# A cross-attention and FFT-FFN layer in fp32: FFN transposes one step earlier, and a written-out order for the last two tiles

## The chip, the cores and the metric

The kernel runs on one core of one Trainium2 chip. The metric is device microseconds from start to end of one execution. A core has five engines that run side by side[...]: TensorE (PE: matmuls and transposes, with weight loads shown as PEld), VectorE (DVE), ScalarE (ACT), GpSimd (POOL) and SyncE (SP, which here only issues DMAs). In the trace each engine works through its instructions in the order in which the program gives them.

## The reference

All data are fp32: x is 2 x 2048 x 512, the encoder's rows are 2 x 128 x 512, and the mask gives each query row 128 keys. In shortened form:

```python
q = layernorm(x) @ wq + bq            # 16 heads of 32
k, v = enc @ wk + bk, enc @ wv + bv
s = (q @ k.T) / sqrt(32) * mask
s = where(s == 0, -1e9, s)
x = x + softmax(s) @ v @ wo + bo
x = x + real(ifft(fft(layernorm(x)) @ (wr + 1j * wi))) + bias
```

The FFT, the complex product and the inverse FFT are linear, so the kernel builds one real 512 x 512 matrix `m_ffn` at its start and each FFN is one product with it.

## The kernel before, in words

The 4096 rows are 8 **groups** of 512 rows, and each group is 4 **tiles** of 128 rows. A tile goes through a **slot**. In slot (i, t), group i's tile t has its scores and softmax computed, while PE fills the time with products of neighbouring groups: queries of group i+1 (chain `q`), the output projection of group i-1 (chain `o`), the FFN of groups i-1 and i-2 (chain `y`). The text calls the group being attended i, the one before it p, the one before that pp, and i+2 is nn.

A **chain** (`chain`, L192) is 4 accumulating 128x512 matmuls; fp32 shows each as two records in the trace, so one chain is 8 records. A product needs its left operand with the contracted dimension on the partitions, so rows are first transposed: `transpose_rows` (L181) is 4 PE transposes of 128x128 into one PSUM bank, and one copy from there to SBUF by ACT or DVE. Three kinds occur: `tp_a` (normalized rows for the queries, copied to `xnT`), `tp_f` (normalized rows for the FFN, copied to `nT`) and `tpw` (softmax weights, in `transposed_weights`, L363, copied to `pt`).

PSUM is dealt out by three pools: `ps_sc` has 2 buffers of two banks for scores (one for each half of the heads), `ps_tp` has 2 banks that take turns for all transposes, `ps_mm` has 2 banks that take turns for chains. A bank can be written again only after the copy or add that reads it.

The softmax of one half of the heads (class `Softmax`, L318) is four steps. `masked` (L328, DVE) multiplies the scores by the mask. `maxima` (DVE) is L335 (the replacement of zeros), L337 (minimum of each head) and L338 (scaling). `exponentials` (L344, ACT) is 8 exponentials. `divided` is the reciprocal L356 on DVE and the product L357 on POOL. The transposes `tpw` of a tile need the product L357 of both halves.

The FFN of a row tile starts when its projection is added to x (`Project.evict`, L428, DVE). Then come `ffn_statistics` (L203 and L204 on DVE, L207 and L208 on POOL, which make `rstd_f`), `ffn_norm` (L211 on DVE, `norm_f`, and L447 on POOL, which adds the bias to x), `ffn_transposes` (PE and a copy to `nT`), and the chain `y` with its final add (L491, DVE) and the store.

Tile hands out buffers and semaphores, but the order is written by hand (`manual_schedule`). The function `slot` (L712) lays a slot out as: scores; `masked` of half 0; adds left over from the slot before (`carried`); the lists `pool` and `early`; `maxima` of half 0; chain 1; the first two `tpw` groups of the tile before; exponentials of half 0; `masked` of half 1; the add of chain 1; `on_a`; `maxima` of half 1; `on_m`; chain 2; `mid_b`; the last two `tpw` groups; exponentials of half 1; `divided` of half 0; the add of chain 2; `on_b`; chain 3; `end`; `divided` of half 1; `on_c`. Everything that a list names goes to its engines' queues at that place. A loop runs groups 1 to 5 through four slots each (group 1's slot 0 is written out before it), then groups 6 and 7 are written out, with their own lists. After the last slot come the last chain `y` of group 6, the `tpw` of the last tile, the context of group 7, its four projections and its four FFNs.

Of the kernel before, what the change touches and what calls it, by code (L numbers as in the profile page):

```python
# [9 lines left out]
FP = mybir.dt.float32  # L10
# [4 lines left out]
P = 128  # L15
# [7 lines left out]
def kernel(  # L23
# [62 lines left out]
    HC = NC // 2  # L86
# [22 lines left out]
    last = ngroups - 1  # L109
# [35 lines left out]
    for b in range(B):  # L145
# [3 lines left out]
        c = b * HC  # L149
# [39 lines left out]
        else:  # L189
            eng.tensor_copy(dst, ps)  # L190

    def chain(name, lhs, rhs, width=D):  # L192

        ps = ps_mm.tile([P, D], FP, tag="mm", name=name)[:, :width]
        for c in range(NC):
            nc.tensor.matmul(  # L196
                ps, lhs(c), rhs(c), start=(c == 0), stop=(c == NC - 1)
            )
        return ps

    def statistics(xt, mv, name):
# [67 lines left out]
    class Queries:  # L269
# [5 lines left out]
        def pe(self):  # L275
            i, g = self.i, self.g
            if i not in qTs:
                qTs[i] = big_tile("qT", 2, f"qT_{i}")
            self.ps = chain(
                f"q_{i}_{g}",  # L280
                lambda c: wq[:, c, g * P : (g + 1) * P],
                lambda c: xnTs[i][:, c, self.first * P :],
                width=GQ - self.first * P,
            )
# [75 lines left out]

    pts = {}

    def transposed_weights(i, t, first, end, eng=None):  # L363
        if t == 0 and first == 0:
            pts[i] = [big_tile("pt", 6, f"pt_{i}_{g}") for g in range(NC)]
        ws = weights[i, t]
        for g in range(first, end):
            ps = ps_tp.tile([P, NR, P], FP, tag="tp", name=f"tpw_{i}_{t}_{g}")
            for r in range(NR):
                nc.tensor.transpose(  # L370
                    ps[:, r, :], ws[r // 2].w[:, (r % 2) * NC + g, :], ident
                )
            dst = pts[i][g][:, :, t * P : (t + 1) * P]
            if eng:
                eng.tensor_copy(dst, ps)
            else:
                nc.scalar.copy(dst, ps)  # L377
# [34 lines left out]
    class Project:  # L412
# [2 lines left out]
        def __init__(self, i, t):  # L415
            self.i, self.t = i, t

        def pe(self):
            i, t = self.i, self.t
            self.ps = chain(  # L420
                f"o_{i}_{t}",
                lambda c: cTs[i][:, c, t * P : (t + 1) * P],
                lambda c: wo[:, c, :],
            )

        def evict(self):
# [5 lines left out]
    def ffn_statistics(i, t):  # L432
        n = f"f{i}_{t}"
        mv = small.tile([P, 2], FP, tag="mvf", name=f"mv_{n}")
        rstd = small.tile([P, 1], FP, tag="rstdf", name=f"rstd_{n}")
        statistics(groups[i][:, t, :], mv, n)
        inverse_deviations(rstd, mv[:, 1:2])
        fstats[i, t] = mv, rstd
# [15 lines left out]
    class Ffn:  # L454
        def __init__(self, i, t):
            self.i, self.t = i, t

        def pe(self):
            nT = nTs.pop((self.i, self.t))
            self.ps = chain(  # L460
                f"y_{self.i}_{self.t}",
                lambda c: nT[:, c, :],
                lambda c: m_ffn[:, c, :],
            )

        def in_halves(self):
# [230 lines left out]
    carried = []  # L697

    def run(job):
        job.pe()  # L700
        job.evict()

    def call(work):
        for f, *args in work:
            f(*args)

    def begin(i, t):
        sc = scores(i, t)
        weights[i, t] = [Softmax(i, t, hf, sc[hf]) for hf in range(2)]
        return weights[i, t]  # L710
# [124 lines left out]
    w = begin(0, 0)  # L835
# [20 lines left out]
    w = begin(0, 1)  # L856
# [21 lines left out]
    w = begin(0, 2)  # L878
# [19 lines left out]
    w = begin(0, 3)  # L898
# [32 lines left out]
    w = begin(1, 0)  # L931
# [29 lines left out]
    for i in range(1, last - 1):  # L961
        p, pp, n, nn = i - 1, i - 2, i + 1, i + 2
        q = [Queries(n, g) for g in range(NC)]
        q_nn = Queries(nn, 0)
        o = [Project(p, t) for t in range(TG)]
        f_p = Ffn(p, 0)
        second = q[1:]
        if i > 1:
            f_pp = [Ffn(pp, t) for t in range(TG)]
            second = [q[2], q[3], f_pp[3]]  # L970

        def if_pp(*work):
            return list(work) if i > 1 else []

        if i > 1:
            load_rows(nn)
            load_mask(n)
            load_residual(p)
            slot(
                i,  # L980
                0,
                [f_pp[1], f_pp[2], q[1]],
                turned=(p, TG - 1),
                early=[(ffn_transposes, pp, 1), (ffn_transposes, pp, 2)],
                pool=[(relative, nn, t, nc.gpsimd) for t in range(TG)],
                on_b=[(ffn_norm, pp, 3), (query_statistics, nn, 0, 2)],
                on_c=[(query_statistics, nn, 2, TG)],
                end=[(context, p, 0, 2)],
            )
        slot(  # L990
            i,
            1,
            second,
            turned=(i, 0),
            early=[(context, p, 2, NC)] + if_pp((ffn_transposes, pp, 3)),
            pool=[(output_bias, p)],
            on_b=[(query_norm, nn, 0), (query_norm, nn, 1)],
        )
        slot(
            i,  # L1000
            2,
            o[:3],
            turned=(i, 1),
            early=[(query_transposes, nn, 0), (query_transposes, nn, 1)],
            on_b=[
                (ffn_statistics, p, 0),
                (query_norm, nn, 2),
                (query_norm, nn, 3),
                (ffn_norm, p, 0),
            ],  # L1010
            on_c=[(ffn_statistics, p, 1)],
        )
        slot(
            i,
            3,
            [o[3], f_p, q_nn],
            turned=(i, 2),
            early=[
                (query_transposes, nn, 2),
                (query_transposes, nn, 3),  # L1020
                (ffn_transposes, p, 0),
            ],
            on_a=[(ffn_statistics, p, 2)],
            on_b=[(ffn_statistics, p, 3), (ffn_norm, p, 1)],
            on_c=[(ffn_norm, p, 2)],
        )


# [2 lines left out]
    i, n, p, pp = last - 1, last, last - 2, last - 3  # L1031
# [3 lines left out]
    o = [Project(p, t) for t in range(TG)]  # L1035
    f = [Ffn(pp, t) for t in range(TG)]
    f_p = [Ffn(p, t) for t in range(TG)]
# [2 lines left out]
        0,  # L1040
        [f[1], f[2], q[1]],
        turned=(p, TG - 1),
        early=[(ffn_transposes, pp, 1), (ffn_transposes, pp, 2)],
        on_b=[(ffn_norm, pp, 3)],
        end=[(context, p, 0, 2)],
    )
# [4 lines left out]
        turned=(i, 0),  # L1051
        soon=True,
        early=[(context, p, 2, NC), (ffn_transposes, pp, 3)],
# [48 lines left out]
    w[1].maxima()  # L1102
    w[1].exponentials()
    w[0].divided()
    o[0].pe()
    carried.append(o[0].evict)
    w[1].divided()
    load_residual(last)
    slot(
        i,  # L1110
        2,
        o[1:],
        turned=(i, 1),
        on_a=[(ffn_statistics, p, 0), (ffn_statistics, p, 1), (ffn_norm, p, 0)],
        on_m=[(ffn_norm, p, 1)],
        end=[(ffn_transposes, p, 0, nc.vector), (ffn_statistics, p, 2)],
    )
    slot(
        i,
        3,  # L1120
        f_p[:3],
        turned=(i, 2),
        early=[(ffn_transposes, p, 1)],
        mid_b=[(ffn_transposes, p, 2)],
        on_a=[(ffn_norm, p, 2), (ffn_statistics, p, 3)],
        on_m=[(ffn_norm, p, 3)],
        end=[(ffn_transposes, p, 3, nc.vector)],
    )
    carried.pop()()
    output_bias(last)  # L1130
    run(f_p[3])
    for g in range(NC):
        transposed_weights(last, TG - 1, g, g + 1, nc.vector if g % 2 else None)
    context(last, 0, NC)
    o = [Project(last, t) for t in range(TG)]
    f = [Ffn(last, t) for t in range(TG)]
# [56 lines left out]
```

## Time and profile before

| what | us |
|---|---|
| median of 3 runs (lowest to highest) | 547.02 (546.65 to 547.3) |
| the profiled execution, its own time | 546.47 |
| its span in the trace | 544.7 |
| PE busy in the span | 528.8 (97%) |
| DVE, ACT, POOL busy | 431.5, 342.9, 329.5 |
| one group in the steady loop (start of slot 0's scores, 325.86 to 387.40) | 61.54 |

The difference between the profiled time and its span, 1.8 us, lies before the first and after the last instruction. Busy PE is modelled from starts, so the better reading is from start to start: in the timeline a chain of 8 records begins 3.44 us before whatever follows it, and a block of 4 transposes 0.44 us. Time beyond such steps is time in which PE waited.

### The profile page before, as it was taken

Reading aid. Unit: us, or ns where it says so; the run is one execution under the profiler, and the core shown is the slowest. Engines: PE = TensorE matmul, PEld = TensorE weight load, DVE = VectorE, ACT = ScalarE, POOL = GpSimd, SP = SyncE. Lnnn points to the kernel's source line nnn. Section 1 sums busy time; section 2 is a strip of 40 time slices with the busy share of each in tenths; the row PEclk is TensorE's granted clock in tenths of the full one; section 3 lists DMA queues with packets and bytes.
Section 4 is the critical chain, followed back from the end, with each engine's and each line's share of the span. In section 5 each row is a group of like instructions: output and inputs, shape, how many; then the busy total and the mean of one; then the engine's idle time right before and its main releaser. Section 6 shows DMA issues by size and latency. Waiting matters only on the chain.

```text
span 544.7 us, 8783 instructions
## 1 busy us (share of the span) xinstructions
PE 528.8 (97%) x3005; PEld 292.7 (54%) x3005; DVE 431.5 (79%) x616; ACT 342.9 (63%) x1300; POOL 329.5 (61%) x268
## 2 busy tenths in 40 slices
PE   8989999999999999999999999999999999998997
PEld 7745566455545554455545555455545555554444
DVE  4798878899887989889887989889857898798251
ACT  3376886776677666666677676666686667756210
POOL 3256759826994469626895369626664466765450
PEclk9999999999999999999999999999999999999999
DMA  8950202000600024000510024000312001201102
GB/s 310 384 213 1 78 15 84 1 0 2 203 31 2 20 81 152 0 21 1 194 40 0 21 62 171 1 21 0 117 40 71 27 20 55 83 1 40 39 0 78
DMA packets 22992, 36.49 MB, mean 67 GB/s; under 512 B 2202, under 2 KB 6562, under 8 KB 22948
## 3 DMA queue, kind: packets, MB, share of 16 engines
q1 hardware_dynamic: 22260, 34.75, 18.4%
q10 hardware_dynamic: 688, 1.18, 0.6%
q8 instruction: 24, 0.39, 0.3%
q14 instruction: 20, 0.16, 0.1%
HBM read 27.53 MB, written 8.39 MB: 66 GB/s over the span
## 4 chain that ended last, share of the span: by engine, by line
PE 79%; DVE 11%; ACT 6%; POOL 1%; issue 1%; DMA 1%; SPq 0%; ACTq 0%; DVEq 0%; POOLq 0%
PE o L196 18%; PE y L196 17%; PE q L196 16%; PE tpw L370 8%; PE sc L309 5%; PE c L392 5%; ACT w L344 4%; DVE w L335 3%; DVE nmax L337 2%; PE tp_f L186 2%; DVE w L328 2%; PE tp_a L186 2%; PE k L535 1%; PE v L196 1%; DMA enc<-in_ctx_dram 1%
## 5 line engine op out<-in xcount | busy, mean ns | idle before, releaser
L344 ACT ACTIVATE w<-w,nmax 128x128 f32<-128x128 f32 x512 | 198.3, 395 | 19.2 <-DVE nmax L338 17.3
L357 POOL TENSOR_TENSOR w<-w,rden 128x1024 f32<-128x1024 f32 x64 | 123.7, 1933 | 120.0 <-DVE rden L356 59.9
L196 PE MATMUL o<-wo,cT 128*128 128x512 f32 x256 | 115.1, 594 | 0.0
L196 PE MATMUL y<-m_ffn,nT 128*128 128x512 f32 x248 | 112.4, 596 | 2.3 <-ACT nT L188 1.2
L196 PE MATMUL q<-xnT,wq 128*128 128x512 f32 (+1 forms) x256 | 112.0, 582 | 2.6 <-ACT qT L287 1.5
L377 ACT COPY pt<-tpw 128x512 f32<-128x512 f32 x122 | 65.6, 587 | 65.2 <-PE tpw L370 65.2
L344 ACT ACTIVATION_READ_ACCUMULATOR w<-w,nmax 128x1 f32 x512 | 99.4, 194 | 0.0
L335 DVE SCALAR_TENSOR_TENSOR w<-w 128x1024 f32<-128x1024 f32 x64 | 89.8, 1404 | 0.9
L328 DVE TENSOR_TENSOR w<-sc,mask 128x1024 f32<-128x1024 f32 x64 | 77.4, 1210 | 10.3 <-PE sc L309 9.9
L337 DVE TENSOR_REDUCE nmax<-w 128x8 f32<-128x1024 f32 x64 | 78.1, 1220 | 2.2
L370 PEld LDWEIGHTS tpw<-ident,w 128*128 128x128 f32 x512 | 59.4, 141 | 34.9 <-issue 29.3
L196 PEld LDWEIGHTS q<-xnT,wq 128*128 128x128 f32 x256 | 46.3, 190 | 48.6 <-issue 40.2
L196 PEld LDWEIGHTS o<-wo,cT 128*128 128x128 f32 x256 | 46.3, 190 | 47.9 <-issue 46.6
L196 PEld LDWEIGHTS y<-m_ffn,nT 128*128 128x128 f32 x248 | 44.7, 190 | 48.7 <-issue 44.8
L370 PE MATMUL tpw<-ident,w 128*128 128x128 f32 x512 | 67.9, 274 | 2.5 <-ACT nT L188 1.0
L447 POOL TENSOR_TENSOR x<-x,bf 128x512 f32<-128x512 f32 x32 | 48.9, 1528 | 18.3 <-DVE norm_f L211 18.3
L356 DVE RECIPROCAL rden<-den 128x8 f32<-128x8 f32 x64 | 12.7, 198 | 45.7 <-ACT w L344 45.7
L408 POOL TENSOR_TENSOR x<-x,bo 128x512 f32<-128x512 f32 x32 | 47.2, 1507 | 0.0
L309 PEld LDWEIGHTS sc<-kT,qT 32*128 32x128 f32 x1024 | 31.5, 186 | 21.0 <-issue 18.8
L228 POOL TENSOR_SCALAR rel<-rows 128x512 f32<-128x512 f32 x26 | 42.0, 1630 | 1.2 <-PE tp_a L186 1.2
L207 POOL TENSOR_SCALAR rstd_f<-mv_f 128x1 f32<-128x1 f32 x32 | 20.0, 625 | 34.8 <-DVE mv_f L204 34.8
L188 ACT COPY nT<-tp_f 128x512 f32<-128x512 f32 x30 | 17.1, 585 | 34.5 <-PE tp_f L186 34.4
(95 smaller groups left out, 535.1 us busy)
## 6 DMA issues: line engine op xcount, KB each, us to landing
rows<-in_x_dram SPq DMA_DIRECT2D x32, 256.0 KB, 4.7
x<-in_x_dram SPq DMA_DIRECT2D x32, 256.0 KB, 4.9
out_dram<-x SPq DMA_DIRECT2D x31, 256.0 KB, 2.0
mask<-in_mask_Bx1xSxS_fk_dram SPq DMA_DIRECT2D x8, 256.0 KB, 5.2
wk<-in_L_xattn_wk_w_dram ACTq DMA_DIRECT2D x2, 512.0 KB, 6.2
wq<-in_L_xattn_wq_w_dram SPq DMA_DIRECT2D x1, 1024.0 KB, 7.2
wr<-n_L_ffn_w_freq_real_dram SPq DMA_DIRECT2D x2, 512.0 KB, 5.2
wi<-n_L_ffn_w_freq_imag_dram SPq DMA_DIRECT2D x2, 512.0 KB, 7.7
```

The lines of the kernel that those rows point to most:

```text
L196: nc.tensor.matmul(ps, lhs(c), rhs(c), start=(c == 0), stop=(c == NC - 1))
L228: eng.tensor_scalar(d, xt, xt[:, 0:1], None, ALU.subtract)
L309: nc.tensor.matmul(sc[r // 2][:, r % 2, g, :], qTs[i][rows, g, t * P : (t + 1) * P], kT[rows, g, b * K : (b + 1) * K], start=True, stop=True,)
L328: nc.vector.tensor_tensor(self.w, self.sc.rearrange("p r g k -> p (r g) k"), self.mrow, ALU.mult)
L335: nc.vector.scalar_tensor_tensor(w, w, 0.0, w, ALU.is_equal, ALU.subtract)
L337: nc.vector.tensor_reduce(self.nmax, w, AX.X, ALU.min)
L344: nc.scalar.activation(w[:, h, :], w[:, h, :], AF.Exp, bias=self.nmax[:, h : h + 1], scale=-UNIT, accum_out=self.den[:, h : h + 1],)
L357: nc.gpsimd.tensor_tensor(w, w, rden.unsqueeze(2).to_broadcast([P, HH, K]), ALU.mult)
L370: nc.tensor.transpose(ps[:, r, :], ws[r // 2].w[:, (r % 2) * NC + g, :], ident)
L377: nc.scalar.copy(dst, ps)
L408: nc.gpsimd.tensor_tensor(xs[:, t, :], xs[:, t, :], bo, ALU.add)
L447: nc.gpsimd.tensor_tensor(xt, xt, bf, ALU.add)
```

## The change

The change has four parts.

1. In the loop, `(ffn_transposes, p, 0)` moves from slot 3's `early` to the end of slot 2, and `(ffn_transposes, pp, 1)` moves from the next group's slot 0 `early` to the end of slot 3 (also for group 6's slot 0). In slot 2 the statistics of tile 0 go from `on_b` to `on_a`, and its norm goes ahead of two query norms. In slot 3 the norm of tile 1 goes ahead of the statistics of tile 3.
2. `chain` takes `between`: work that is issued after its second matmul. For the last tiles it puts a whole `ffn_transposes` in the middle of a chain.
3. Slots 2 and 3 of group 7 are written out instead of using `slot`: `masked` of tile 2 now stands ahead of `divided` of tile 1's second half, and `maxima`, exponentials, norms and statistics stand in another order.
4. The last tile's four `tpw` groups go into the two score buffers (four banks) instead of through the two banks of `ps_tp`.

No operation is added or removed; SP's queue of DMA issues is the same, in the same order. The diff, cut to its core:

```diff
+    def chain(name, lhs, rhs, width=D, between=()):
...
+            if c == HC - 1:
+                call(between)
...
             ps = (
+                banks[g]
+                if banks
+                else ps_tp.tile([P, NR, P], FP, tag="tp", name=f"tpw_{i}_{t}_{g}")
             )
...
# loop, slot 0 (and the same in group 6)
-                early=[(ffn_transposes, pp, 1), (ffn_transposes, pp, 2)],
+                early=[(ffn_transposes, pp, 2)],
# loop, slot 2
-            on_b=[
-                (ffn_statistics, p, 0),
-                (query_norm, nn, 2),
-                (query_norm, nn, 3),
-                (ffn_norm, p, 0),
-            ],
+            on_a=[(ffn_statistics, p, 0)],
+            on_b=[(ffn_norm, p, 0), (query_norm, nn, 2), (query_norm, nn, 3)],
             on_c=[(ffn_statistics, p, 1)],
+            end=[(ffn_transposes, p, 0)],
# loop, slot 3
-            early=[
-                (query_transposes, nn, 2),
-                (query_transposes, nn, 3),
-                (ffn_transposes, p, 0),
-            ],
+            early=[(query_transposes, nn, 2), (query_transposes, nn, 3)],
             on_a=[(ffn_statistics, p, 2)],
-            on_b=[(ffn_statistics, p, 3), (ffn_norm, p, 1)],
+            on_b=[(ffn_norm, p, 1), (ffn_statistics, p, 3)],
             on_c=[(ffn_norm, p, 2)],
+            end=[(ffn_transposes, p, 1)],
# group 7 (i = 7, p = 6), from the first projection on
-    o[0].pe()
-    carried.append(o[0].evict)
-    w[1].divided()
-    load_residual(last)
-    slot(i, 2, o[1:], turned=(i, 1),
-        on_a=[(ffn_statistics, p, 0), (ffn_statistics, p, 1), (ffn_norm, p, 0)],
-        on_m=[(ffn_norm, p, 1)],
-        end=[(ffn_transposes, p, 0, nc.vector), (ffn_statistics, p, 2)])
-    slot(i, 3, f_p[:3], turned=(i, 2),
-        early=[(ffn_transposes, p, 1)],
-        mid_b=[(ffn_transposes, p, 2)],
-        on_a=[(ffn_norm, p, 2), (ffn_statistics, p, 3)],
-        on_m=[(ffn_norm, p, 3)],
-        end=[(ffn_transposes, p, 3, nc.vector)])
-    carried.pop()()
+    run(o[0])
+    ffn_statistics(p, 0)
+    load_residual(last)
+    old = w
+    w = begin(i, 2)
+    w[0].masked()
+    old[1].divided()
+    o[1].pe()
+    w[0].maxima()
+    ffn_norm(p, 0)
+    transposed_weights(i, 1, 0, HC)
+    w[0].exponentials()
+    w[1].masked()
+    o[1].evict()
+    ffn_statistics(p, 1)
+    w[1].maxima()
+    o[2].pe()
+    transposed_weights(i, 1, HC, NC)
+    w[1].exponentials()
+    ffn_norm(p, 1)
+    w[0].divided()
+    o[2].evict()
+    ffn_statistics(p, 2)
+    o[3].pe(between=[(ffn_transposes, p, 0, nc.vector)])
+    ffn_transposes(p, 1)
+    w[1].divided()
+    w = begin(i, 3)
+    w[0].masked()
+    o[3].evict()
+    ffn_statistics(p, 3)
+    ffn_norm(p, 2)
+    f_p[0].pe()
+    w[0].maxima()
+    transposed_weights(i, 2, 0, HC)
+    w[0].exponentials()
+    w[1].masked()
+    f_p[0].evict()
+    f_p[1].pe(between=[(ffn_transposes, p, 2, nc.vector)])
+    ffn_norm(p, 3)
+    w[1].maxima()
+    transposed_weights(i, 2, HC, NC)
+    f_p[1].evict()
+    w[0].divided()
+    w[1].exponentials()
+    f_p[2].pe(between=[(ffn_transposes, p, 3, nc.vector)])
+    f_p[2].evict()
+    w[1].divided()
     output_bias(last)
     run(f_p[3])
+    free = [
+        ps_sc.tile([P, 2, NC, K], FP, tag="sc", name=f"tpw_last_{hf}")
+        for hf in range(2)
+    ]
+    banks = [free[g // 2][:, g % 2] for g in range(NC)]
     for g in range(NC):
-        transposed_weights(last, TG - 1, g, g + 1, nc.vector if g % 2 else None)
+        transposed_weights(
+            last, TG - 1, g, g + 1, nc.vector if g % 2 else None, banks
+        )
```

More of the change, by code (lines that the diff above doesn't have):

```diff
@@ L190, in transpose_rows, with call @@
             eng.tensor_copy(dst, ps)
-    def chain(name, lhs, rhs, width=D):
+    def call(work):
+        for f, *args in work:
+            f(*args)
+    def chain(name, lhs, rhs, width=D, between=()):
         ps = ps_mm.tile([P, D], FP, tag="mm", name=name)[:, :width]
@@ L361, with transposed_weights @@
     pts = {}
-    def transposed_weights(i, t, first, end, eng=None):
+    def transposed_weights(i, t, first, end, eng=None, banks=None):
         if t == 0 and first == 0:
@@ L367, in transposed_weights @@
         for g in range(first, end):
-            ps = ps_tp.tile([P, NR, P], FP, tag="tp", name=f"tpw_{i}_{t}_{g}")
+            ps = (
+                banks[g]
+                if banks
+                else ps_tp.tile([P, NR, P], FP, tag="tp", name=f"tpw_{i}_{t}_{g}")
+            )
             for r in range(NR):
@@ L416, in __init__, with pe @@
             self.i, self.t = i, t
-        def pe(self):
+        def pe(self, between=()):
             i, t = self.i, self.t
@@ L423, in pe @@
                 lambda c: wo[:, c, :],
+                between=between,
             )
@@ L456, in __init__, with pe @@
             self.i, self.t = i, t
-        def pe(self):
+        def pe(self, between=()):
             nT = nTs.pop((self.i, self.t))
@@ L463, in pe @@
                 lambda c: m_ffn[:, c, :],
+                between=between,
             )
@@ L701, in run @@
         job.evict()
-    def call(work):
-        for f, *args in work:
-            f(*args)
     def begin(i, t):
@@ L1042 @@
         turned=(p, TG - 1),
-        early=[(ffn_transposes, pp, 1), (ffn_transposes, pp, 2)],
+        early=[(ffn_transposes, pp, 2)],
         on_b=[(ffn_norm, pp, 3)],
@@ L1104 @@
     w[0].divided()
-    o[0].pe()
-    carried.append(o[0].evict)
-    w[1].divided()
-    load_residual(last)
[L1109 to L1113, printed above, removed]
-        on_a=[(ffn_statistics, p, 0), (ffn_statistics, p, 1), (ffn_norm, p, 0)],
-        on_m=[(ffn_norm, p, 1)],
[L1116 to L1122, printed above, removed]
-        early=[(ffn_transposes, p, 1)],
-        mid_b=[(ffn_transposes, p, 2)],
-        on_a=[(ffn_norm, p, 2), (ffn_statistics, p, 3)],
-        on_m=[(ffn_norm, p, 3)],
-        end=[(ffn_transposes, p, 3, nc.vector)],
-    )
-    carried.pop()()
+    run(o[0])
[23 more added lines that the diff above has]
+    ffn_transposes(p, 1)
+    w[1].divided()
+    w = begin(i, 3)
[19 more added lines that the diff above has]
+    w[1].divided()
     output_bias(last)
     run(f_p[3])
+    free = [
[3 more added lines that the diff above has]
+    banks = [free[g // 2][:, g % 2] for g in range(NC)]
     for g in range(NC):
-        transposed_weights(last, TG - 1, g, g + 1, nc.vector if g % 2 else None)
+        transposed_weights(
+            last, TG - 1, g, g + 1, nc.vector if g % 2 else None, banks
+        )
     context(last, 0, NC)
```

## The prediction

> **What bounds the kernel now.** I read the page's busy shares and its chain that ended last, then who waited for whom on PE, then PE's timeline around each wait.
>
> ```profile
> span 544.7 us, 8783 instructions
> PE 528.8 (97%) x3005; PEld 292.7 (54%) x3005; DVE 431.5 (79%) x616; ACT 342.9 (63%) x1300; POOL 329.5 (61%) x268
> ```
>
> PE is busy 97% of the span and makes up 79% of the chain. No PE instruction is added or removed, so the change can give only waits: the idle time of PE is 544.7 - 528.8 = 15.9 us over the whole kernel. PE's waits, longest in total first, name where these are:
>
> ```profile
> PE tp_f L186 <- ACT xnT L188: 1.2, 5, 0.2
> PE y L196 <- ACT nT L188: 1.2, 5, 0.2
> PE tpw L370 <- ACT nT L188: 1.0, 3, 0.4
> PE y L196 <- DVE nT L190: 1.0, 2, 0.8
> PE tpw L370 <- POOL w L357: 0.7, 1, 0.7
> ```
>
> The first two come five times each, 0.24 us at a time, once per group of the loop. Since ends are modelled, I size them from starts in PE's timeline (start, busy, what, count):
>
> ```profile
> 310.78 1.17 PE L309 MATMUL sc<-kT,qT 32*128 32x128 f32 x32
> 311.89 1.09 PE L186 MATMUL tp_a<-ident,rel 128*128 128x128 f32 x8
> 313.22 0.66 PE L186 MATMUL tp_f<-ident,norm_f 128*128 128x128 f32 x4 [0.24 <-ACT xnT L188]
> 313.71 3.60 PE L196 MATMUL o<-wo,cT 128*128 128x512 f32 x8
> ...
> 325.86 1.17 PE L309 MATMUL sc<-kT,qT 32*128 32x128 f32 x32
> 326.96 1.09 PE L186 MATMUL tp_f<-ident,norm_f 128*128 128x128 f32 x8
> 328.30 3.70 PE L196 MATMUL y<-m_ffn,nT 128*128 128x512 f32 x8 [0.24 <-ACT nT L188]
> ```
>
> Two transpose blocks after scores take 0.93 (at 359.25 `tp_a`, chain `o` at 360.18), but 1.33 and 1.34 here: 0.40 us of waiting each. The third block waits for the copy that frees its `ps_tp` bank, and the chain `y` for its own `nT`. After the second, `y` also runs 0.10 long (328.30 to 331.83, 3.53 against 3.44).
>
> In group 7's slots 2 and 3 the waits are larger:
>
> ```profile
> 489.52 0.38 PE L370 MATMUL tpw<-ident,w 128*128 128x128 f32 x2
> 490.63 0.88 PE L370 MATMUL tpw<-ident,w 128*128 128x128 f32 x6 [0.73 <-POOL w L357]
> 491.35 3.60 PE L196 MATMUL y<-m_ffn,nT 128*128 128x512 f32 x8
> 495.44 0.63 PE L186 MATMUL tp_f<-ident,norm_f 128*128 128x128 f32 x4 [0.50 <-DVE norm_f L211]
> 496.95 0.66 PE L370 MATMUL tpw<-ident,w 128*128 128x128 f32 x4 [0.44 <-ACT nT L188]
> 502.27 3.70 PE L196 MATMUL y<-m_ffn,nT 128*128 128x512 f32 x8 [0.79 <-DVE nT L190]
> 507.08 1.20 PE L370 MATMUL tpw<-ident,w 128*128 128x128 f32 x8 [0.24 <-ACT pt L377]
> ```
>
> From start to start against 3.44 per chain and 0.87 per 8 transposes, these lose 0.95, 0.66, 0.66, 0.95 + 0.10 and 0.66. The `tp_f` at 485.14 (0.85 for 0.49) adds 0.36, and the `tpw` at 474.60 (1.16 for 0.87) adds 0.29. In all 4.6 us.
>
> **What the Trainium skill says.** "SBUF — State Buffer", section Who interferes with whom: DVE and POOL share one port pair by an exclusive lock, which POOL instructions take, and on DVE the 2-port modes and instructions with two SBUF inputs; whoever starts first blocks the other fully. The trace agrees, both ways (DVE, DVE, POOL):
>
> ```profile
> 489.36 2.30 DVE L335 SCALAR_TENSOR_TENSOR w<-w 128x1024 f32<-128x1024 f32 x1
> 326.40 0.50 DVE L211 TENSOR_SCALAR norm_f<-x,mv_f,rstd_f 128x512 f32<-128x512 f32 x1
> 326.63 2.02 POOL L357 TENSOR_TENSOR w<-w,rden 128x1024 f32<-128x1024 f32 x1 [0.16 <-DVE rden L356]
> ```
>
> At 489.36, L335, which takes 1.21 alone, runs 1.1 us past the end of a POOL product at 490.58: DVE was held. At 326.63 a product (1.90 alone) is held 0.12 by a norm that started 0.23 earlier. L338 is held too (1.09 for 0.17 where L408 runs on POOL). Statistics, `masked` and PSUM adds show no hold. "Perfetto Trace Analysis", section Optimization Strategy: a gap that keeps returning on the saturated engine can mean too few buffers. Here true of slot 3's wait (a `ps_tp` bank), not of slot 0's (the data).
>
> **Loop, part by part.** I lay the moved work into group 4's slots 2 and 3 and group 5's slot 0.
>
> *What goes.* Slot 3, scores to `o`, was 313.71 - 310.78 = 2.93. Now: `tp_f` 0.44 after `o`'s third chain, scores 1.10, two `tp_a` 0.93 = 2.47. Gain 0.46. Slot 0 was 328.30 - 325.86 + 0.10 = 2.54; now `tp_f` 0.44, scores 1.10, one `tp_f` 0.49 = 2.03. Gain 0.51. The 0.09 that a chain loses ahead of scores falls on `tp_f` instead (443.92 to 444.45, 0.53). Sum 0.97 x 5 groups = **4.85**.
>
> *Is the data there a slot earlier?* Slot 2, tile 0: its add ends at 303.97, so statistics end at 304.8. They push `maxima` of half 1 back 0.8, to 307.35; ACT starts those exponentials at 307.98 after its `pt` copies, so 0.6 covers it. The reciprocal comes at 307.3 (was 306.89), the product runs from 307.6 to 309.5, the norm waits behind it for the lock and ends at 309.8. PE is ready for it at 310.69: 0.9 to spare. On POOL, `rstd_f` goes ahead of the first product and has 3 us of idle time before it. The two query norms come after the norm; at worst the bias add L447 gets in between (1.27), so the second ends at 311.8, against PE's need at 312.8. The reciprocal of half 1, behind it on DVE, slips 0.6 at most; its product then ends by 314.0, and `tpw` needs it at 316.7. ACT: exponentials end 311.2, the `nT` copy 312.0; its bank is wanted at 312.8.
>
> Slot 3, tile 1: the norm moves ahead of the statistics, but now starts while half 0's product holds the lock (322.4 to 324.4), so it ends at 324.6; PE wants it at 325.3: 0.7 to spare. POOL's bias add follows, tile 2's norm ends 326.4, wanted at 326.9. The last product ends about 0.3 later than before (329.0), wanted at 330.9. The copy of `nT` for tile 1 (ACT, after the exponentials and the query copy, 326.3 to 326.9) is wanted at 327.4. In slot 1 DVE has 1.2 and 2.0 us of idle time (before 354.39 and 359.01), so lateness doesn't add up over groups. SP is passed by nothing.
>
> **Group 7.** All times as before, without the loop's shift.
>
> 1. `masked` of tile 2 starts at 471.5 instead of 472.87, ahead of the reciprocal that waits for ACT until 472.75. But now L335 follows that reciprocal at 472.87, and the product of half 1, due at 473.10, meets its lock. By the norm's example it is held until 0.15 before L335's end (474.08): 0.85 lost, end 475.85. PE's `tpw`, which got the product at 475.0, waits 0.85 longer. **-0.85**.
> 2. From there PE runs `o`, `tpw`, `o` with `tp_f` inside, `tp_f`, scores, `y` without a wait: tile 0's norm is ready at 476.6 (wanted 482.6), tile 1's at 482.4 (wanted 484.8), tile 0's `nT` by DVE at 484.7 (wanted 486.4), the product of tile 2's half 1 at 488.5 (wanted 490.0). That removes 0.36 and 0.95. **+1.3**. `y` after the first `tpw` starts at 490.9.
> 3. `tp_f` 2 inside `y`: norm ready at 489.9, wanted 492.6. **+0.66**.
> 4. Second `tpw`: its last group takes the bank of `tp_f` 2, whose copy by DVE stands behind L338, `masked` and an add, and ends at 495.5 against 495.2. Lost 0.3 of 0.66. **+0.36**.
> 5. `tp_f` 3 inside the third `y`, its `nT` at 499.9, just when the last `y` may start: **+1.05** (0.95 + 0.10, which the first `y` keeps).
> 6. Last `tpw`: four banks free since `masked`, so 4 x 0.44 = 1.75 instead of 2.41: **+0.66**. But DVE is now the late one: `masked` 486.7, L338 held behind L447 to 493.1, then `masked`, add, copy, norm, L335 to L338 until 498.5, exponentials 3.1, reciprocal and product 2.4: 504.1, against PE at 503.4. **-0.7**, less the part that group 0 does first (0.15): -0.55.
>
> Sum: -0.85 + 1.3 + 0.66 + 0.36 + 1.05 + 0.66 - 0.55 = **2.6**. A transpose block inside a chain does not occur in the trace. The nearest is `tp_f` between two chains (522.24 to 522.68, 0.44), which I take. A gain is excluded, since the same records run; a loss is bounded by the 0.10 that a chain shows when it starts after a break, x 3 = 0.3. A transpose into a score bank I take at 0.44 as well, since `ps_tp` has the same form; bounds 0 and 0.05 a group.
>
> **The number.** 4.85 + 2.6 = 7.45 off the profiled execution: span 544.7 to 537.25, time 546.47 to 539.0. The median lies 0.55 above it: **539.6**.
>
> **Rivals.**
> - *No lock at 473.10* (POOL takes the port first, or L338 slips in): terms 1 and 6 vanish, +1.4, 538.2. For it: the two are 0.23 us apart. Against: L211 won by that same 0.23. Chance 0.17.
> - *Waits come back in the loop*: `nT` of tile 1 and the norms have only 0.5 to 0.9 to spare. If half of the loop's gain and a third of group 7's go: 2.4 + 1.7 = 4.1, 542.9. Against: PE's pattern repeats to 0.02 us in all five groups. Chance 0.15. If all goes, the change does not do what it says and the time is 547.0: 0.03.
> - *Slower*: one more POOL multiplication ahead of each norm. The norms of tiles 0 and 1 give way at the lock, and at the end of slots 2 and 3 PE stands at the head of its queue with scores, softmax and everything behind it. One product (1.90) more costs 1.90 - 0.9 + 1.90 - 0.7 = 2.2 a group, 11 in all; less 7.45, 550.6. It decides once the norms are some 1.5 us later than worked out. For it: the queue is 61% busy and both norms stand behind a product. Against: after that product POOL has nothing ready but what waits for these norms. Chance 0.05.
>
> Forecast 0.60. About 0.2% (1.1 us) is what a measurement of this kernel can tell from no change, given runs 0.65 apart. Faster: 0.60 + 0.17 + 0.15 = 0.92; same 0.03; slower 0.05. The range reaches below to all waits gone (4.85 + 4.6 = 9.45, 537.6) and above to 542.6, most of the second rival.
>
> **What would show it.** Right: no 0.24 waits on ACT at slots 3 and 0, groups 60.6 apart; in group 7 a product near 2.75 long after L335; the last `tpw` 1.75 plus about 0.5 of wait on POOL. Wrong: PE waits for `norm_f` ahead of scores, or L335 at 2 us or more behind that product instead, or chains with a block inside longer than 3.88.

## The result and the profile after

The changed kernel takes 541.11 us (median of 4 runs, 540.94 to 541.26) against 547.11 for the kernel before in the same measurement: a ratio of 0.9891, 95% interval 0.9874 to 0.9909. That is 6.0 us less; the forecast was 7.45 less. In the profiled executions the span fell by 5.7, from 544.7 to 539.0. In the experiments below, one run of e5 and two of e6 show a mean granted clock of 0.996 instead of 0.999 to 1.000, and are 1.5 to 2.4 us longer than the other runs of their kernel.

The diff shifts lines in the changed kernel: L335 is now L341, L337 and L338 are L343 and L344, L328 is L334, L356 and L357 are L362 and L363, L370 is L380, L377 (the copy to `pt` by ACT) is L387, L196 is L200, L211 is L217, L309 is L315, L392 is L402.

First the page, span and busy time by engine:

```profile
span 539.0 us, 8776 instructions
PE 526.0 (98%) x3005; PEld 293.4 (54%) x3005; DVE 437.2 (81%) x617; ACT 342.3 (64%) x1299; POOL 330.0 (61%) x268
```

PE runs the same 3005 instructions and is still the bound. Its idle time went from 15.9 to 13.0, and its busy time fell by 2.8 although it does the same work. That is why waits have to be sized from starts: part of the waits was shown as busy time of the instruction ahead of them. DVE has one instruction more and ACT one less (616 and 1300 before), because the diff also moves one copy between them, which the list of four parts does not say: the copy of `tp_f` 2 in group 7, made by ACT before, now gets `nc.vector`.

Then who waited for whom on PE (total, times, longest), of which I show the lines that belong to this change:

```profile
PE tpw_last L380 <- ACT pt L387: 1.4, 2, 0.7
...
PE tpw L380 <- POOL w L363: 1.0, 1, 1.0
...
PE tpw L380 <- ACT nT L188: 0.5, 2, 0.3
...
PE tpw_last L380 <- POOL w L363: 0.3, 1, 0.3
```

The two lines of 1.2 us in five waits each are gone, and so are those of `y` on `nT` by DVE and of `tp_f` on `norm_f`. (These two did not lead the whole list before, as the prediction's excerpt suggests: `q` on `qT` with 1.5 and `busy` on `ident` with 1.3, once each, stood above them, and both are still there.) But a new line stands near the top that the prediction does not have: the last tile's transposes wait twice for an ACT copy.

PE's timeline in group 4's slots 2 and 3 and at group 5's slot 0 (start, busy, what, count):

```profile
308.06 0.60 PE L186 MATMUL tp_f<-ident,norm_f 128*128 128x128 f32 x4
308.59 1.17 PE L315 MATMUL sc<-kT,qT 32*128 32x128 f32 x32
309.69 1.09 PE L186 MATMUL tp_a<-ident,rel 128*128 128x128 f32 x8
310.62 3.60 PE L200 MATMUL o<-wo,cT 128*128 128x512 f32 x8
...
322.67 0.60 PE L186 MATMUL tp_f<-ident,norm_f 128*128 128x128 f32 x4
323.20 1.17 PE L315 MATMUL sc<-kT,qT 32*128 32x128 f32 x32
324.31 0.66 PE L186 MATMUL tp_f<-ident,norm_f 128*128 128x128 f32 x4
324.80 3.60 PE L200 MATMUL y<-m_ffn,nT 128*128 128x512 f32 x8
```

Nothing in brackets stands behind any of these lines, so none shows idle time. From scores to `o` it is 310.62 - 308.59 = 2.03, and the `tp_f` ahead of them takes 0.53. A group of the steady loop lasts 383.79 - 323.20 = 60.59 instead of 61.54.

And group 7, from slot 2's first `tpw` to the context:

```profile
470.04 0.38 PE L380 MATMUL tpw<-ident,w 128*128 128x128 f32 x2
471.38 0.87 PE L380 MATMUL tpw<-ident,w 128*128 128x128 f32 x6 [0.96 <-POOL w L363]
472.09 3.60 PE L200 MATMUL o<-wo,cT 128*128 128x512 f32 x8
475.53 1.04 PE L380 MATMUL tpw<-ident,w 128*128 128x128 f32 x8
476.40 1.88 PE L200 MATMUL o<-wo,cT 128*128 128x512 f32 x4
478.12 0.60 PE L186 MATMUL tp_f<-ident,norm_f 128*128 128x128 f32 x4
478.56 1.88 PE L200 MATMUL o<-wo,cT 128*128 128x512 f32 x4
480.27 0.60 PE L186 MATMUL tp_f<-ident,norm_f 128*128 128x128 f32 x4
...
498.38 0.38 PE L380 MATMUL tpw_last<-ident,w 128*128 128x128 f32 x2
499.04 0.44 PE L380 MATMUL tpw_last<-ident,w 128*128 128x128 f32 x2 [0.28 <-POOL w L363]
500.15 1.09 PE L380 MATMUL tpw_last<-ident,w 128*128 128x128 f32 x8 [0.68 <-ACT pt L387]
501.93 0.66 PE L380 MATMUL tpw_last<-ident,w 128*128 128x128 f32 x4 [0.68 <-ACT pt L387]
502.51 3.69 PE L402 MATMUL c<-pt,v 128*32 128x512 f32 x32
```

The first `tpw` takes 472.09 - 470.04 = 2.05 against 0.87 without a wait. The chain with a transpose block inside takes 480.27 - 476.40 = 3.87. The last 16 transposes take 502.51 - 498.38 = 4.13, where four groups without a wait are 1.75. Groups 0 and 2 are copied out by ACT:

```profile
499.52 0.58 ACT L387 COPY pt<-tpw_last 128x512 f32<-128x512 f32 x1 [2.80 <-PE tpw_last L380]
501.29 0.59 ACT L387 COPY pt<-tpw_last 128x512 f32<-128x512 f32 x1 [1.18 <-PE tpw_last L380]
```

These copies end at 500.10 and 501.88, and groups 1 and 3 start 0.05 later each, at 500.15 and 501.93. Each waits for the copy of the group that shares its score buffer.

From slot 2's scores to the context, group 7 went from 38.25 (469.96 to 508.21) to 37.11 (465.40 to 502.51): 1.1 less. What comes after the context's start is 36.5 long in both kernels.

### The profile page after: what moved, and what is told of

It is laid out like the page before. It is cut to its first block, busy times and chain, and to the rows that moved or that the text cites. A ratio compares the mean times of both kernels' runs of the same rounds, so it can differ in the third digit from the quotient of the medians.

```text
span 539.0 us, 8776 instructions
## 1 busy us (share of the span) xinstructions
PE 526.0 (98%) x3005; PEld 293.4 (54%) x3005; DVE 437.2 (81%) x617; ACT 342.3 (64%) x1299; POOL 330.0 (61%) x268
## 3 DMA queue, kind: packets, MB, share of 16 engines
q10 hardware_dynamic: 688, 1.18, 0.6%
## 4 chain that ended last, share of the span: by engine, by line
PE 83%; DVE 10%; ACT 3%; POOL 2%; issue 1%; POOLq 0%; ACTq 0%; DVEq 0%
PE o L200 20%; PE q L200 16%; PE y L200 16%; PE tpw L380 9%; PE c L402 6%; PE sc L315 5%; PE tp_f L186 3%; PE tp_a L186 3%; ACT w L350 2%; DVE w L341 2%; DVE w L334 2%; DVE nmax L343 2%; POOL w L363 1%; PE k L547 1%; PE v L200 1%; DVE st_a L209 1%
## 5 line engine op out<-in xcount | busy, mean ns | idle before, releaser
L363 POOL TENSOR_TENSOR w<-w,rden 128x1024 f32<-128x1024 f32 x64 | 123.9, 1935 | 84.9 <-DVE rden L362 69.3
L200 PE MATMUL o<-wo,cT 128*128 128x512 f32 x256 | 115.3, 594 | 0.0
L200 PE MATMUL q<-xnT,wq 128*128 128x512 f32 (+1 forms) x256 | 112.0, 582 | 2.6 <-ACT qT L293 1.5
L200 PE MATMUL y<-m_ffn,nT 128*128 128x512 f32 x248 | 112.0, 594 | 0.2 <-DVE x L503 0.2
L387 ACT COPY pt<-tpw 128x512 f32<-128x512 f32 x120 | 64.3, 587 | 60.0 <-PE tpw L380 60.0
L341 DVE SCALAR_TENSOR_TENSOR w<-w 128x1024 f32<-128x1024 f32 x64 | 88.8, 1387 | 0.9
L334 DVE TENSOR_TENSOR w<-sc,mask 128x1024 f32<-128x1024 f32 x64 | 77.5, 1212 | 13.9 <-PE sc L315 13.6
L343 DVE TENSOR_REDUCE nmax<-w 128x8 f32<-128x1024 f32 x64 | 78.1, 1220 | 2.2
L380 PEld LDWEIGHTS tpw<-ident,w 128*128 128x128 f32 x496 | 57.7, 141 | 33.6 <-issue 29.3
L200 PEld LDWEIGHTS q<-xnT,wq 128*128 128x128 f32 x256 | 46.3, 190 | 48.6 <-issue 40.2
L200 PEld LDWEIGHTS o<-wo,cT 128*128 128x128 f32 x256 | 46.2, 190 | 47.5 <-issue 46.1
L200 PEld LDWEIGHTS y<-m_ffn,nT 128*128 128x128 f32 x248 | 44.6, 190 | 44.6 <-issue 43.8
L380 PE MATMUL tpw<-ident,w 128*128 128x128 f32 x496 | 65.2, 273 | 2.0 <-POOL w L363 1.0
L458 POOL TENSOR_TENSOR x<-x,bf 128x512 f32<-128x512 f32 x32 | 50.4, 1576 | 15.0 <-DVE norm_f L217 15.0
L213 POOL TENSOR_SCALAR rstd_f<-mv_f 128x1 f32<-128x1 f32 x32 | 18.1, 564 | 67.0 <-DVE mv_f L210 67.0
L315 PEld LDWEIGHTS sc<-kT,qT 32*128 32x128 f32 x1024 | 31.5, 186 | 15.1 <-issue 12.8
L362 DVE RECIPROCAL rden<-den 128x8 f32<-128x8 f32 x64 | 12.6, 197 | 31.9 <-ACT w L350 31.7
```

The costliest lines, as they stand in the source:

```text
L200: nc.tensor.matmul(ps, lhs(c), rhs(c), start=(c == 0), stop=(c == NC - 1))
L315: nc.tensor.matmul(sc[r // 2][:, r % 2, g, :], qTs[i][rows, g, t * P : (t + 1) * P], kT[rows, g, b * K : (b + 1) * K], start=True, stop=True,)
L334: nc.vector.tensor_tensor(self.w, self.sc.rearrange("p r g k -> p (r g) k"), self.mrow, ALU.mult)
L341: nc.vector.scalar_tensor_tensor(w, w, 0.0, w, ALU.is_equal, ALU.subtract)
L343: nc.vector.tensor_reduce(self.nmax, w, AX.X, ALU.min)
L363: nc.gpsimd.tensor_tensor(w, w, rden.unsqueeze(2).to_broadcast([P, HH, K]), ALU.mult)
```

## The experiments

Each is compared with runs of the kernel before on the same chip, whose median was 546.92 beside e1 to e4, 547.18 beside e5 to e7 and 546.96 beside e8 and e9. Gains are against these. Diffs are against the changed kernel unless the text says otherwise.

### Which half brings what

**e1_loop_only** keeps part 1 of the change (the loop) and takes group 7's order and the last `tpw` as before. Its edit, cut to the core:

```diff
-    run(o[0])
-    ffn_statistics(p, 0)
...
+    o[0].pe()
+    carried.append(o[0].evict)
...
+    slot(
...
+        end=[(ffn_transposes, p, 3, nc.vector)],
+    )
...
-            last, TG - 1, g, g + 1, nc.vector if g % 2 else None, banks
...
+        transposed_weights(last, TG - 1, g, g + 1, nc.vector if g % 2 else None)
```

> Part 1 of the change alone: the loop's transposes of tiles 0 and 1 a slot earlier, groups 6 and 7 as before. Theory (the loop gives what start-to-start times say): 4.7 to 4.9 us faster than before, about 542.3, each loop group 60.6 us long, no PE wait on ACT ahead of the moved blocks. Rival (the loop and the tail overlap, so the parts don't add): clearly less than 4.5, or the sum of this run and the next differs from the whole change by more than 0.7.

Measured: 542.23 us, ratio 0.9915 (0.99 to 0.993), 4.7 less; span 539.9, 4.8 less. Its group 7 repeats the old waits to 0.01 us.

**e2_tail_only** is the reverse: the loop as before, parts 2 to 4 as changed.

```diff
-                early=[(ffn_transposes, pp, 2)],
+                early=[(ffn_transposes, pp, 1), (ffn_transposes, pp, 2)],
...
-            end=[(ffn_transposes, p, 0)],
...
+                (ffn_transposes, p, 0),
...
-            end=[(ffn_transposes, p, 1)],
```

> Parts 2 to 4 alone: chains with transposes inside, the written-out slots 2 and 3 of group 7, and the last weights in score banks, with the loop and group 6 as before. Theory (the shortfall of 1.5 us against the prediction lies in the last transposes of weights): 1.1 to 1.3 us faster than before, about 545.9, the last 16 weight transposes still about 4.1 us from their first to the context. Rival (it was lost in the loop or at its seam with group 7): 2.4 to 2.8 faster.

Measured: 545.79, ratio 0.9981 (0.9974 to 0.9988), 1.1 less; span 1.1 less; from slot 2's scores to the context 37.11, the very figure of the whole change. The two halves add up: 4.7 + 1.1 = 5.8 against 6.0. So the loop paid nearly what was forecast (4.85), and nearly all of the shortfall lies in group 7.

**e9_slot0_only** halves the loop again: of part 1 only the move of tile 1's block is made, in the kernel before.

```diff
-                early=[(ffn_transposes, pp, 1), (ffn_transposes, pp, 2)],
+                early=[(ffn_transposes, pp, 2)],
...
-            on_b=[(ffn_statistics, p, 3), (ffn_norm, p, 1)],
+            on_b=[(ffn_norm, p, 1), (ffn_statistics, p, 3)],
...
+            end=[(ffn_transposes, p, 1)],
```

> The kernel before with one move of part 1 only: tile 1's FFN transposes go from the next group's slot 0 to the end of slot 3, and the norm of tile 1 goes ahead of the statistics of tile 3; nothing else. Theory (each of the two moved blocks takes its own wait away, one for the data and one for a bank): per group 0.51 us less, 2.5 us in all, time 0.9953 of before, about 544.5; PE's 0.24 us waits ahead of y at slot 0 gone, those of slot 3's tp_f on the bank's copy still there, five times. Rival (the two waits are one chain, so that one move either takes both away or only shifts the wait): 4.7 less, or nothing.

Measured: 544.54, ratio 0.9957 (0.994 to 0.9974), 2.4 less; a group lasts 61.06, which is 0.48 less. The waits on PE still hold slot 3's line, five times as before, while that of `y` on ACT is gone:

```profile
PE tp_f L186 <- ACT xnT L188: 1.2, 5, 0.2
```

This move takes only its own wait away and gives about half of the loop's gain. The other move was not run alone; what is left for it of e1's 4.7 is 2.3, about the same.

### The last tile's transposes

**e3_old_ring** is the change without part 4: the last four groups go through the two `ps_tp` banks again.

```diff
-    banks = [free[g // 2][:, g % 2] for g in range(NC)]
...
-            last, TG - 1, g, g + 1, nc.vector if g % 2 else None, banks
...
+        transposed_weights(last, TG - 1, g, g + 1, nc.vector if g % 2 else None)
```

> The change without its part 4: the last tile's weight transposes go through the two transpose banks again. Theory (two groups that share one score tile wait for each other's copy, 0.84 us twice; the ring of two banks waits 0.40 to 0.45 once or twice, as before): faster than the change by 0.9 to 1.3 us, about 540.0; from the first of these transposes to the context about 2.9 us instead of 4.13. Rival (the 4.13 us come from PSUM score banks or a late product and not from sharing a tile): the same as the change within 0.3, or slower by 0.4 to 0.7, which is what part 4 was worth in the prediction.

Measured: 539.73, ratio 0.987 (0.9855 to 0.9885), 7.2 less than before; span 537.9. From `tpw` to the context 2.91 (498.50 to 501.41) instead of 4.13. The score banks, meant to free these transposes, cost 1.2 us.

**e4_four_tiles** gives each group a buffer of its own: two `ps_tp` buffers and one bank of each score buffer.

```diff
-    banks = [free[g // 2][:, g % 2] for g in range(NC)]
+    banks = [
+        ps_tp.tile([P, NR, P], FP, tag="tp", name="tpw_last_0"),
+        free[0][:, 0],
+        ps_tp.tile([P, NR, P], FP, tag="tp", name="tpw_last_2"),
+        free[1][:, 0],
+    ]
```

> The change with its four last weight groups in four different PSUM tiles: two transpose banks and one bank of each score buffer. Same banks in use, no tile shared. Theory (the wait comes from sharing a tile): from the first transpose to the context 1.75 plus the wait for the product of half 1 of 0.45 to 0.5, so 2.3 us instead of 4.13; faster than the change by 1.6 to 1.9 us, about 539.4. Rival (a score bank is slow to write, or the copies are late): the groups in the score banks still start 0.84 us after the one before, gain under 0.9.

Measured: 539.38, ratio 0.9863 (0.9847 to 0.988), 7.5 less than before, so 1.5 more than the change gains. The profiled execution is the fastest of four, 539.1, and its span of 537.1 is 1.9 less than the change's. PE's timeline:

```profile
498.24 0.38 PE L380 MATMUL tpw_last<-ident,w 128*128 128x128 f32 x2
498.90 0.44 PE L380 MATMUL tpw_last<-ident,w 128*128 128x128 f32 x2 [0.28 <-POOL w L363]
499.18 0.60 PE L380 MATMUL tpw_last_sc<-ident,w 128*128 128x128 f32 x4
499.61 0.60 PE L380 MATMUL tpw_last<-ident,w 128*128 128x128 f32 x4
500.05 0.60 PE L380 MATMUL tpw_last_sc<-ident,w 128*128 128x128 f32 x4
500.58 3.69 PE L402 MATMUL c<-pt,v 128*32 128x512 f32 x32
```

Groups start 0.44 apart, the product's wait stays, the two on ACT are gone: 500.58 - 498.24 = 2.34, near the 1.75 and about 0.5 that the prediction gave for the change itself. That is 1.79 less than the change's 4.13.

**e8_alternate** keeps the change's four banks and moves only which group uses which, so that neighbours don't share a buffer.

```diff
-    banks = [free[g // 2][:, g % 2] for g in range(NC)]
+    banks = [free[g % 2][:, g // 2] for g in range(NC)]
```

> The whole change, but the last tile's four groups of weight transposes alternate between the two score buffers: groups 0 and 2 lie in the two banks of one, groups 1 and 3 in those of the other. The same four banks, the same order on PE. Theory (a wait for a whole buffer: a group waits for the copy out of the other group that shares its buffer, though that lies in another bank): groups 0 and 1 now start without a wait for each other, group 2 waits for the copy of group 0, which ends about 1.28 us after group 0's last start step (0.44 + 0.84), so 0.40 after group 1's end instead of 0.84 after its own partner's; group 3 waits as little or not at all. From the first of these transposes to the context about 2.8 us instead of 4.13; time 1.2 to 1.3 us less than the change, about 539.8. Rival (the second bank of a score buffer costs the wait, or a copy by ACT out of score banks is slow in itself): still two waits near 0.84 and about 4.1 us, time as the change.

Measured: 539.75, ratio 0.987 (0.9855 to 0.9885), 7.2 less than before; span 537.8.

```profile
498.43 0.38 PE L380 MATMUL tpw_last<-ident,w 128*128 128x128 f32 x2
499.09 0.87 PE L380 MATMUL tpw_last<-ident,w 128*128 128x128 f32 x6 [0.28 <-POOL w L363]
500.20 1.20 PE L380 MATMUL tpw_last<-ident,w 128*128 128x128 f32 x8 [0.24 <-ACT pt L387]
501.33 3.70 PE L402 MATMUL c<-pt,v 128*32 128x512 f32 x32
```

One wait for a copy is left, ahead of group 2, and the whole takes 2.90. The same banks, the same copies and the same order on PE cost 1.2 us less, and the two score buffers behave like the two `ps_tp` banks of e3. So neither the second bank nor the copy is slow: a group waits until the other group in its buffer has been copied out, though it writes another bank. The Trainium skill ("PSUM — Partial Sum Buffer", section PSUM bank collisions raise a hardware error) says that accesses of two engines to different banks run clean, and that even on a collision the hardware does not stall. The traces fit: the wait follows the buffer and not the bank. That the cause is a semaphore which the framework sets for the whole buffer is inferred from this; no run shows it directly.

### The lock at the start of slot 2

**e5_mask_between** lets the mask product of tile 2's half 1 follow the reciprocal, so that a DVE instruction with one SBUF input stands where L341 stood.

```diff
     w[0].masked()
     old[1].divided()
     o[1].pe()
+    w[1].masked()
     w[0].maxima()
     ffn_norm(p, 0)
     transposed_weights(i, 1, 0, HC)
     w[0].exponentials()
-    w[1].masked()
```

> The change with one DVE order swapped in group 7's slot 2: the masking of half 1 now stands between the reciprocal of tile 1's half 1 and L341 (the replacement of zeros, L335 before). Theory (L341 takes the shared port 0.23 us ahead of the POOL product and holds it 0.86): the product at that place takes 1.90 instead of 2.76, the weight transposes behind it 1.2 instead of 2.05, and since the scores of tile 3 follow 0.85 sooner, and DVE's chain starts from them, the end comes 0.7 to 0.9 sooner, about 540.3. Rival (DVE's chain in slot 2 is what sets the end, so the product only waits elsewhere): product 1.90, but the last weight transposes wait 0.85 longer for their product and the time stays within 0.3 of the change.

Measured: 540.63, ratio 0.9884 (0.9866 to 0.9903), 6.6 less than before, so 0.6 more than the change gains; span 538.4. The change's DVE and POOL, then those of e5:

```profile
468.34 1.23 DVE L341 SCALAR_TENSOR_TENSOR w<-w 128x1024 f32<-128x1024 f32 x1
...
468.56 2.76 POOL L363 TENSOR_TENSOR w<-w,rden 128x1024 f32<-128x1024 f32 x1 [0.40 <-DVE rden L362]
```

```profile
469.75 2.11 DVE L341 SCALAR_TENSOR_TENSOR w<-w 128x1024 f32<-128x1024 f32 x1
...
468.88 1.90 POOL L363 TENSOR_TENSOR w<-w,rden 128x1024 f32<-128x1024 f32 x1 [0.40 <-DVE rden L362]
```

In the change the product starts 0.22 behind L341 and takes 2.76; in e5 it is first and takes 1.90, and now L341 takes 2.11 instead of 1.23. PE's `tpw` falls from 2.05 to 1.18 and slot 2's scores to the context from 37.11 to 36.26, by 0.85. The wait of the last transposes on their product does not grow in return (0.30 idle, in the change 0.28), so the rival fails. The span fell by 0.6 only, because 0.32 was lost ahead of everything that the edit touches: the very first scores begin at 64.28 instead of 63.96, and e5's list has a wait of 0.4 for the first DMA that the change's has not. The change's four runs lie 0.3 apart and e5's 2.4, so the times alone do not settle this one; the trace does.

### How near the loop is to the slower case

**e6_norm_last** puts slot 2's norm of tile 0 back behind the two query norms on DVE.

```diff
-            on_b=[(ffn_norm, p, 0), (query_norm, nn, 2), (query_norm, nn, 3)],
+            on_b=[(query_norm, nn, 2), (query_norm, nn, 3), (ffn_norm, p, 0)],
```

> The change with the norm of tile 0 behind the two query norms in the loop's slot 2, as it stood before the change. Theory (that norm has 0.8 us to spare ahead of PE: it ends at 307.27 in the trace of the change and PE turns to its transposes at 308.06): behind two query norms of 0.46 each it ends 0.9 later, PE waits 0.1 to 0.2 in each of five groups, and the time rises by 0.5 to 1.0, to about 541.9. Rival (the slower one of the prediction: a norm that gives way costs PE a whole POOL product, and the slot behind it): 1.5 or more a group, over 548. Rival (the place doesn't matter, as the norm is early anyway): the same within 0.3.

Measured: 544.34, ratio 0.9945 (0.9929 to 0.9961), 2.8 less than before: by medians 3.2 of the change's 6.0 us are lost. Two of the four runs are of the longer kind named in the result. The profiled one, 543.59, is not; it is 3.6 less than before, so 2.4 are lost, and its span, 541.4, is 2.4 above the change's. The trace puts 2.1 of that in the loop: from slot 2 to slot 3 takes 14.92 instead of 14.62 in four groups, and 15.66 instead of 14.75 in the first. Another 0.35 lies ahead of the loop, where the first scores start at 64.31 instead of 63.96. The 2.1 is more than the theory's figure and far from the slower rival's. DVE and the POOL product in group 4, the change, then e6 (`rel` are the two query norms):

```profile
305.42 1.85 DVE L217 TENSOR_SCALAR norm_f<-x,mv_f,rstd_f 128x512 f32<-128x512 f32 x1
307.19 1.95 DVE L217 TENSOR_SCALAR rel<-rel,mv,rstd 128x512 f32<-128x512 f32 x2
...
305.09 1.90 POOL L363 TENSOR_TENSOR w<-w,rden 128x1024 f32<-128x1024 f32 x1 [0.97 <-DVE rden L362]
```

```profile
307.27 2.30 DVE L217 TENSOR_SCALAR rel<-rel,mv,rstd 128x512 f32<-128x512 f32 x2
309.50 0.53 DVE L217 TENSOR_SCALAR norm_f<-x,mv_f,rstd_f 128x512 f32<-128x512 f32 x1
...
306.94 1.90 POOL L363 TENSOR_TENSOR w<-w,rden 128x1024 f32<-128x1024 f32 x1 [0.97 <-DVE rden L362]
```

Whichever norm comes first starts 0.33 behind the product and is held until 0.28 after its end (306.99 in the change, 308.84 in e6). In the change `norm_f` ends at 307.27 and PE turns to it at 308.06. In e6 it ends at 310.03, PE is through with its chain at 309.91, and `tp_f` starts at 310.18: 0.12 late, and then 0.15 from the norm's end to the start on PE. This 0.15 I had left out of the spare time. In the first group the norm ends at 127.38 and `tp_f` starts 0.15 later, a whole us behind a PE that was ready at 126.52. PE's list of waits names only this one of the five.

### A version with both repairs

**e7_best** has e5's order, e4's four buffers, and transposes half 0 of all four groups before half 1 of any, since half 0's product is ready earlier.

```diff
+    for hf in range(2):
+        for g in range(NC):
+            for r in (2 * hf, 2 * hf + 1):
+                nc.tensor.transpose(
+                    banks[g][:, r, :], ws[hf].w[:, (r % 2) * NC + g, :], ident
+                )
+            if hf:
...
```

> The change with four tiles for the last weight groups, the masking between reciprocal and L341, and the last 16 weight transposes ordered by half of the heads (eight that need only the first product, then eight that need the second). Theory (the three gains are separate waits on PE): 1.8 for the tiles, 0.85 for the port, and 0.3 to 0.45 because eight transposes now cover the wait for the last product: 538.0 to 538.4. Rival (with PE sooner the last product is the bound and gives back what the port gave): 539.0 or more.

Measured: 538.42 (538.05 to 538.66), ratio 0.9837 (0.9823 to 0.985), span 536.1: 8.8 less than before, and the fastest of all. The last transposes wait for nothing, 499.57 - 497.64 = 1.93:

```profile
497.64 0.38 PE L1172 MATMUL tpw_last<-ident,w 128*128 128x128 f32 x2
...
499.17 0.38 PE L1172 MATMUL tpw_last_sc<-ident,w 128*128 128x128 f32 x2
499.57 3.69 PE L402 MATMUL c<-pt,v 128*32 128x512 f32 x32
```

## Why the prediction was right, and where it was not

The direction, the place and, save for one step, the mechanism held: PE's waits were the whole gain, and 541.1 lies inside the range. The size was 1.45 too large by medians and 1.75 by spans. The time still lies in the range because the loop, the larger term, came within 0.15; in group 7 less than half of the forecast came. Step by step, measured from start to start:

| step | predicted | measured | how |
|---|---|---|---|
| loop, five groups | 4.85 | 4.7 | 0.95 a group; e1 alone 4.7 |
| 1, product held by L335's lock | -0.85 | -0.89 | first `tpw` 2.05, before 1.16 |
| 2, no wait to slot 3's first `tpw` | +1.3 | +1.36 | `tp_f` blocks 1.38 to 0.97, `tpw` 1.82 to 0.87 |
| 3, `tp_f` 2 inside `y` | +0.66 | +0.68 | 4.56 to 3.88 |
| 4, second `tpw` | +0.36 | +0.67 | 1.54 to 0.87 |
| 5, `tp_f` 3 inside `y` | +1.05 | +1.05 | 8.36 to 7.31 |
| 6, last `tpw` with its DVE term | +0.11 | -1.72 | 2.41 to 4.13 |

- **Loop.** Right. Slots 3 and 0 both lost their waits, and e9 shows that slot 0's is separate (0.48 a group, forecast 0.51). The first of the five groups gives about 0.1 less: its norm ends at 126.13 and PE, ready at 126.18, starts at 126.28.
- **Term 1.** Right, and shown by e5: the product was forecast at 2.75 and took 2.76. What the Trainium skill ("SBUF — State Buffer", section Who interferes with whom) says of the exclusive lock carried this term, and e5 agrees from the other side: L341, which came second there, took 2.11. The "no lock" rival did not come. e5, where the product goes first, is worth 0.85 and not 1.4: there the last `tpw` still wait for their product.
- **Terms 2, 3 and 5.** Right. The unknown among them, transposes inside an open chain, costs 3.87 less 3.44, so 0.43 to 0.44, with no loss for the chain that is taken up again.
- **Term 4.** 0.31 too small. The second `tpw`, at 490.19, waits for nothing. I had its last group behind a DVE copy of `tp_f` 2 that was to end 0.3 too late. In the trace that copy stands where I put it on DVE, but runs from 489.68 to 490.35, and the group starts at 490.63. What came sooner is L344 ahead of it. I had it held by the bias add on POOL until 493.1, which is 488.5 in this trace (its times lie 4.57 earlier here). The bias add ended at 488.01 and L344 at 488.03, 0.5 sooner.
- **Term 6, the step that failed.** It said "four banks free", so 1.75, and -0.55 for the product that is now late. The second half held: the wait on the product is 0.45. The first did not. The banks were free, but two groups share each buffer, and each second group waits for the copy of the first, 0.84 beyond its step, twice, with a slower step (by 0.06) behind each wait: 4.13 instead of 2.30. e4 and e8 show it. What the text on the kernel says of a bank, that it can be written again only after the copy that reads it, held here for the whole buffer. e3 shows the two old banks in between, 2.91, so part 4, forecast at +0.66, cost 1.2. With e4's 2.34 the change would have gained 1.8 more by the trace, 1.5 by medians.
- **The sum.** Group 7 fell 1.45 short, 1.15 for 2.6: term 6 is 1.83 of it, term 4 gives 0.31 back, the others change it by less than 0.1 together. The loop is 0.15 short, and 0.12 is lost ahead of it, where the first scores start at 63.96 instead of 63.84. That is 7.45 forecast and 5.7 measured in the span.
- **The other rivals.** Waits did not come back in the loop, save that 0.1. The slower case did not come: the norms had 0.79 and 0.82 to spare (forecast 0.9 and 0.7), of which 0.15 is needed to pass on. e6 shows that it was near enough to matter and what it costs to cross the line: 0.3 a group for a norm that comes 0.9 later against PE, and 0.9 in the first group, where there was nothing to spare.

## What to carry to other kernels

On a saturated engine, size a wait from start to start and not from the idle column, and look at each stage alone: here ten equal small waits in a loop were worth four times a rewritten tail. Count the buffers that are handed out, not the banks: here two uses of one buffer took turns even though they touched different banks, and the second started only when the first had been copied out. When two engines share a lock and start close together, 0.22 us here, put a neighbour that does not take the lock between them, and let the one that the bound waits for go first.

## What the runs showed of the hardware that I had not expected

A chain can be left after its second matmul for four transposes into another bank and taken up again at no cost at all: 1.72 + 0.44 + 1.72, each record within 0.01 us of its usual step. The prediction had to borrow the 0.44 from a place between two chains, and bounded the loss at 0.1 each time. A norm's end on DVE and the start of the transposes that wait for it on PE are 0.14 to 0.15 us apart in all five groups of e6, and 0.15 in the change where PE waits for one at 126.28.
